# A decoder layer on one core: the first attention scores computed in 32x32 blocks instead of 32x128 strips

## The chip, the cores and the metric

The kernel runs on one core of one Trainium2 chip. Its time is the device time of one execution in microseconds (us); the figure for a version is the median over its runs. A core has five engines that run side by side: TensorE (PE in the profile; its weight loads are listed apart as PEld), VectorE (DVE), ScalarE (ACT), GpSimd (POOL) and SyncE (SP, which here issues the DMAs). A score is a number from a product of queries and keys; PSUM is the memory that TensorE writes to, SBUF the one that it reads from.

## The reference

One decoder layer over 128 sequences of 128 positions and width 256: self-attention, cross-attention over a context, and a feed-forward part with ternary weights, each behind a layer norm and added to x.

```python
x = x + attn(layernorm(x), Wq, bq, Wk, bk, Wv, bv, Wo, bo)             # 16 heads of 16
x = x + xattn(layernorm(x), ctx, ctx, mask, wq, wk, wv, wo, biases)    # 16 heads of 16
x = x + ffn(layernorm(x), W_fc, ln_w, ln_b, W_proj)                    # 256 -> 1024 -> 256

# both attentions, for one sequence and head
scores = Q @ K.T / sqrt(16)
scores = where(mask == 0, 1e-09, scores)      # cross-attention only; one mask for all sequences
out = softmax(scores) @ V
```

All inputs and the output are float32.

## The kernel before

The sequences are worked in 32 groups of 4. Each sequence passes through self-attention and through cross-attention; the kernel calls one sequence in one of them a row, so there are 256 rows, 128 self and 128 cross, four of each in turn.

Scores are computed twice in a row. The first scores have the queries on the partitions; only the largest of each query and head is taken from them, so that the exponentials can be shifted. The second scores have the keys on the partitions; they are exponentiated and multiplied with the values. The change touches the first scores.

The steps of a row, in the order in which `attention` (L680) issues them:

- `maxima` (L542): the first scores of the following row, and their maxima. 16 heads lie as 4 strips of 32 partitions (r), 2 chunks (o) and 2 heads in each strip (e). `qt` holds the queries as columns, 128 partitions x 2 chunks x 512 tokens; `kt` holds the keys of the two heads of a strip in two copies, each with the other head's rows set to zero, so one product of 32 rows gives 2 heads x 128 keys. For each o and r, L562 multiplies 32 rows x 128 queries (`qt[strip, o, tok]`, the weights that are loaded) with 32 rows x 256 columns of keys: 8 products, into a score tile of 128 queries, in two PSUM tiles of two banks each, `s[0]` for strips 0 and 1 and `s[1]` for 2 and 3. In a cross row, L551 first writes -1e30 where a key is masked: sixteen bf16 products of 32 rows and 32 columns (an identity) with 512 columns of `never`, one for each strip r and block of 32 queries c; L562 then adds onto them. DVE takes the maxima of the two tiles (L573) and lays them out as `negm` (L579, L584).
- `outputs` (L656): the exponentials of the row before, times the values: 16 products of 128 rows and 32 columns (L665), copied out by ACT (L668).
- `transposed_scores` (L611): the second scores, 16 products of 32 rows and 128 columns (L620), in the same two PSUM tiles as the first scores (pool `ps_s`, two buffers).
- `transposed_maxima` (L587): the maxima of the following row, transposed (L589) and laid out for the second scores (L594, or L604 and L606).
- `weights` (L637): in a cross row the maxima are added by 16 more products (L644); ACT takes the exponentials (L653).

Between these steps stand the steps of other groups: projections of queries, keys and values (L266, L278), output projections (`po`, L278), transposes (L246, L414), the feed-forward products (L385, L437). A string of letters, `ORDER` (L50), fixes how they alternate: "A" is one piece of `attention`, and "n", "k", "c", "f" are pieces of the preparation of self-attention, of the cross keys, of cross-attention and of the feed-forward part. The program issues its instructions in that order, and each engine takes its own in order, so TensorE's sequence is fixed by hand.

The score tiles pass from step to step: first scores (PE), maxima (DVE), second scores (PE), exponentials (ACT), first scores of the next row. Each product that is first in a PSUM tile waits until the reader before has finished: the first product of strip 0 for `s[0]`, the first of strip 2 for `s[1]`.

A float32 product is one call in the program and two instruction pairs (a weight load and a matmul) on the chip; a bf16 or fp32r product is one pair. The instruction stream has the two pairs of a product one behind the other.

## Time and profile before

| | before |
|---|---|
| median of 3 runs | 2844.08 us (2841.91 to 2845.41) |
| the profiled execution | 2845.54 us |
| its span, first to last instruction | 2843.5 us |
| mean granted TensorE clock | 0.98 |
| matmuls and weight loads | 32797 each |
| first scores (L562): matmuls, union of their time | 4096, 301.2 us |
| the mask's products (L551): matmuls, union of their time | 2048, 64.8 us |
| first scores' maxima (L573, DVE): instructions, mean | 512, 1215 ns |
| exponentials (L653, ACT): instructions, mean | 512, 1023 ns |
| instruction fetches (queue q8) | 259 pieces, 4.24 MB |

How to read a group line: the source line, engine and operation, then the tile written and the tiles read, for a matmul its rows*columns in the array, the partitions x elements that stream, and the count; behind the first bar the busy time (us) and the mean duration of one (ns); behind the second the engine's idle time just before these instructions, and what ended it. A matmul's duration overlaps with its neighbours', because matmuls are pipelined; what a group costs is read from the start of its first matmul to the start of the next group's. A line of the chain that ended last gives a start (us), a length (us) and the work. A timeline line gives the start and the length of a merged group, and how many instructions of it had begun in the stretch asked for.

### The profile page before, as it was taken

The numbers are of one execution on the slowest core, as the hardware profiler recorded it, in microseconds if no ns is written. First come the engines' busy times: TensorE is split into PE (matmuls) and PEld (weight loads), VectorE is DVE, ScalarE is ACT, GpSimd is POOL, SyncE is SP. The second block draws the span as 40 slices with busy tenths as digits, with TensorE's granted clock in tenths as the row PEclk, the third lists the DMA queues.
The fourth block names the chain that finished last, engine by engine and source line by source line (L and its number), as shares of the span: only waits on it lengthen the run. The fifth ranks groups of instructions, "written<-read, shape, count | busy, mean of one in ns | idle before, by whom it ended". The sixth has DMA issues, their size and how long they took to land.

```text
span 2843.5 us, 76860 instructions
## 1 busy us (share of the span) xinstructions
PE 2723.7 (96%) x32797; PEld 1965.4 (69%) x32797; DVE 2045.6 (72%) x3788; ACT 1546.9 (54%) x2369; POOL 1371.8 (48%) x1425
## 2 busy tenths in 40 slices
PE   4789999999999999999999999999999999999985
PEld 2456777777777777777777777777777777777664
DVE  4457777787777778777777877777777777787663
ACT  0245555655655565555556556555655655566443
POOL 1225455554545555454545545454544545455343
PEclk8799999999999999999999999999999999999988
DMA  2112211211221121122112112211211221121111
GB/s 82 31 32 48 55 37 43 56 44 44 56 55 33 47 55 40 47 55 55 33 47 55 40 47 55 56 32 49 55 40 47 55 54 32 49 52 33 43 24 31
DMA packets 110948, 131.38 MB, mean 46 GB/s; under 512 B 32657, under 2 KB 69393, under 8 KB 110609
## 3 DMA queue, kind: packets, MB, share of 16 engines
q1 hardware_dynamic: 110608, 126.48, 18.2%
q8 instruction: 259, 4.24, 0.6%
q14 instruction: 81, 0.66, 0.1%
HBM read 71.91 MB, written 18.87 MB: 32 GB/s over the span
## 4 chain that ended last, share of the span: by engine, by line
PE 93%; DVE 3%; DMA 1%; POOL 1%; issue 1%; ACT 1%; SPq 0%; POOLq 0%; ACTq 0%; DVEq 0%
PE st L620 10%; PE s L562 10%; PE av L665 9%; PE py L437 9%; PE po L278 9%; PE ph L385 8%; PE pv L278 8%; PE pq L266 8%; PE pk L266 8%; PE pg L414 4%; PE pt L246 3%; PE st L644 3%; PE s L551 2%; PE pn L589 1%; DVE mx L573 1%
## 5 line engine op out<-in xcount | busy, mean ns | idle before, releaser
L573 DVE TENSOR_REDUCE mx<-s 128x8 f32<-128x1024 f32 x512 | 600.7, 1215 | 73.7 <-PE s L562 71.5
L653 ACT ACTIVATE w_t<-st 128x1024 f32<-128x1024 f32 x512 | 496.6, 1023 | 223.5 <-PE st L620 195.6
L223 POOL TENSOR_SCALAR rstd<-agg 128x4 f32<-128x4 f32 (+1 forms) x160 | 38.1, 238 | 1172.2 <-DVE agg L218 1170.3
L228 POOL TENSOR_SCALAR xn<-x,agg,rstd 128x256 f32<-128x256 f32 x384 | 464.2, 1221 | 10.0
L630 DVE COPY_PREDICATED_SCALAR st<-masked_t,masked_score 128x1024 f32 x256 | 315.7, 1279 | 64.5 <-PE st L620 61.0
L422 ACT ACTIVATE g<-pg,ln_w 128x256 fp32r<-128x256 f32 x512 | 211.4, 477 | 214.4 <-PE pg L414 211.0
L668 ACT COPY raw<-av 128x512 f32<-128x512 f32 x256 | 150.0, 586 | 302.9 <-PE av L665 302.6
L562 PE MATMUL s<-kt,qt 32*128 32x256 f32 x4096 | 301.2, 406 | 1.7 <-ACT w_t L653 1.7
L356 POOL TENSOR_TENSOR o_raw<-o_raw,factors 128x256 f32<-128x256 f32 x256 | 178.8, 726 | 252.5 <-DMA factors<-by_head 196.6
L665 PEld LDWEIGHTS av<-w_t,v 128*32 128x32 f32 x8192 | 211.6, 110 | 118.0 <-issue 26.0
L665 PE MATMUL av<-w_t,v 128*32 128x128 f32 x8192 | 281.2, 278 | 7.2 <-DVE negm_t L606 1.5
L228 POOL TENSOR_SCALAR g<-g,agg,rstd 128x1024 f32<-128x1024 f32 x64 | 276.8, 4324 | 6.7
L385 PE MATMUL ph<-w_fc,xn 128*128 128x512 f32 x1024 | 275.1, 411 | 1.2 <-ACT g L392 1.2
L437 PE MATMUL py<-w_proj,g 128*128 128x256 f32 x2048 | 272.2, 289 | 0.3 <-DVE g L424 0.2
L437 PEld LDWEIGHTS py<-w_proj,g 128*128 128x128 f32 x2048 | 254.9, 194 | 14.7 <-issue 9.6
L562 PEld LDWEIGHTS s<-kt,qt 32*128 32x128 f32 x4096 | 189.1, 187 | 108.1 <-issue 58.3
L424 DVE SCALAR_TENSOR_TENSOR g<-pg,ln_w,g 128x256 fp32r<-128x256 f32 x512 | 216.8, 476 | 32.0 <-ACT g L422 30.0
L385 PEld LDWEIGHTS ph<-w_fc,xn 128*128 128x128 f32 x1024 | 188.6, 192 | 55.2 <-DVE g L228 9.6
L314 DVE COPY v<-pv 128x512 f32<-128x512 f32 x128 | 86.3, 674 | 149.5 <-PE pv L278 149.5
L594 DVE SCALAR_TENSOR_TENSOR q_max<-pn,max_rows,qt 128x256 f32<-128x256 f32 x256 | 110.6, 474 | 111.8 <-PE pn L589 111.8
L392 ACT ACTIVATE g<-ph 128x512 f32<-128x512 f32 x256 | 146.2, 597 | 65.0 <-PE ph L385 64.2
L360 DVE TENSOR_TENSOR x<-x,po 128x512 f32<-128x512 f32 x128 | 87.5, 684 | 120.2 <-PE po L278 120.2
(113 smaller groups left out, 4748.6 us busy)
## 6 DMA issues: line engine op xcount, KB each, us to landing
o_raw<-raw SPq DMA_DIRECT2D x512, 64.0 KB
factors<-by_head SPq DMA_DIRECT2D x128, 256.0 KB
x<-in_x_dram SPq DMA_DIRECT2D x32, 512.0 KB
ctx_t<-in_ctx_t_dram SPq DMA_DIRECT2D x32, 512.0 KB
out_dram<-x SPq DMA_DIRECT2D x32, 512.0 KB
sums<-raw SPq DMA_DIRECT2D x128, 16.0 KB
by_head<-r SPq DMA_DIRECT2D x64, 32.0 KB
raw<-in_w_fc_t_dram SPq DMA_DIRECT2D x1, 1024.0 KB
```

What stands on the lines that cost most here:

```text
L228: engine.tensor_scalar(dst[:, j], src[:, j], agg[:, j, 0:1], rstd[:, j : j + 1], ALU.subtract, ALU.mult)
L266: nc.tensor.matmul(out, w[:, c, o * P : (o + 1) * P], src_t[:, c], start=(c == 0), stop=(c == CC - 1))
L278: nc.tensor.matmul(rows[:, j], src_t[:, c, (j0 + j) * P : (j0 + j + 1) * P], w[:, c], start=(c == 0), stop=(c == CC - 1),)
L385: nc.tensor.matmul(ph, xn_parts[i][:, c, (j0 + j) * P : (j0 + j + 1) * P], w_fc[:, c, n * 512 : (n + 1) * 512], start=((i, c) == terms[0]) ...
L424: nc.vector.scalar_tensor_tensor(parts[1][:, f0 + f], pieces[:, f], scales[f], parts[0][:, f0 + f].bitcast(F32), ALU.mult, ALU.subtract,)
L437: nc.tensor.matmul(rows[:, j], parts[i][:, f, j * P : (j + 1) * P], w_proj[:, f], start=((i, f) == terms[0]), stop=((i, f) == terms[-1]),)
L562: nc.tensor.matmul(s[r // 2][:, r % 2, 2 * o : 2 * o + 2], qt[strip, o, tok], kt[strip, o, :, tok], start=(stage == "self"), stop=True, sk ...
L573: nc.vector.tensor_reduce(mx[:, 2 * half : 2 * half + 2], s[half], AX.X, ALU.max, negate=True)
L620: nc.tensor.matmul(s[r // 2][:, r % 2, n], kt[strip, n // 2, n % 2, tok], added[strip, n // 2, n % 2] if stage == "self" else qt[strip, n ...
L630: nc.vector.copy_predicated(s[half].rearrange("p r n q -> p (r n) q"), masked_t[:, None, :].to_broadcast([P, 8, P]), masked_score[:, :, No ...
L653: nc.scalar.activation(w_t[:, 2 * half : 2 * half + 2], s[half], AF.Exp)
L665: nc.tensor.matmul(av[32 * r : 32 * r + 32, n], v[:, j, head : head + 32], w_t[:, r, n], start=True, stop=True)
```

## The change

The 8 products of 32 rows and 128 queries become 32 products of 32 rows and 32 queries: a loop over c, the block of 32 queries, is added around the loop over r, as L551's products already have it, and both now take their slices from one list, `BLOCKS`. Each product loads 32 columns of `qt` as weights and streams the same 256 columns of keys, into 32 partitions of the score tile. The order is: for each o, for each c, for each r. L551's products keep their operands and order. Everything else stays.

```diff
+BLOCKS = [
+    (r, slice(r * 32, (r + 1) * 32), c, slice(c * 32, (c + 1) * 32)) for c in range(S4) for r in range(S4)
+]
...
         if stage == "cross":
-            for c in range(S4):
-                for r in range(S4):
-                    strip = slice(r * 32, (r + 1) * 32)
-                    nc.tensor.matmul(
-                        s[r // 2][c * 32 : (c + 1) * 32, r % 2],
-                        ident_b[strip],
-                        never[strip, c, None, :].to_broadcast([32, 4, P]),
...
+            for r, strip, c, block in BLOCKS:
+                nc.tensor.matmul(
+                    s[r // 2][block, r % 2],
+                    ident_b[strip],
+                    never[strip, c, None, :].to_broadcast([32, 4, P]),
...
         for o in range(CC):
-            for r in range(S4):
-                strip = slice(r * 32, (r + 1) * 32)
+            for r, strip, c, block in BLOCKS:
+                queries = slice(j * P + block.start, j * P + block.stop)
                 nc.tensor.matmul(
-                    s[r // 2][:, r % 2, 2 * o : 2 * o + 2],
-                    qt[strip, o, tok],
+                    s[r // 2][block, r % 2, 2 * o : 2 * o + 2],
+                    qt[strip, o, queries],
                     kt[strip, o, :, tok],
                     start=(stage == "self"),
                     stop=True,
```

More of the change, by code (lines that the diff above doesn't have):

```diff
@@ L547, in maxima @@
         if stage == "cross":
-            for c in range(S4):
-                for r in range(S4):
-                    strip = slice(r * 32, (r + 1) * 32)
-                    nc.tensor.matmul(
-                        s[r // 2][c * 32 : (c + 1) * 32, r % 2],
-                        ident_b[strip],
-                        never[strip, c, None, :].to_broadcast([32, 4, P]),
-                        start=True,
-                        stop=False,
-                        skip_group_check=True,
-                    )
+            for r, strip, c, block in BLOCKS:
[3 more added lines that the diff above has]
+                    never[strip, c, None, :].to_broadcast([32, 4, P]),
+                    start=True,
+                    stop=False,
+                    skip_group_check=True,
+                )
         for o in range(CC):
-            for r in range(S4):
-                strip = slice(r * 32, (r + 1) * 32)
+            for r, strip, c, block in BLOCKS:
+                queries = slice(j * P + block.start, j * P + block.stop)
                 nc.tensor.matmul(
-                    s[r // 2][:, r % 2, 2 * o : 2 * o + 2],
-                    qt[strip, o, tok],
+                    s[r // 2][block, r % 2, 2 * o : 2 * o + 2],
+                    qt[strip, o, queries],
                     kt[strip, o, :, tok],
```

## The prediction

> **What bounds the kernel now.** I read the page's busy row and slices first, then the busy time by stretches, the chain that ended last, and the timeline around one row of scores.

> ```profile
> PE 2723.7 (96%) x32797; PEld 1965.4 (69%) x32797; DVE 2045.6 (72%) x3788; ACT 1546.9 (54%) x2369; POOL 1371.8 (48%) x1425
> ...
> PE   4789999999999999999999999999999999999985
> ...
> PEclk8799999999999999999999999999999999999988
> ...
> PE 93%; DVE 3%; DMA 1%; POOL 1%; issue 1%; ACT 1%; SPq 0%; POOLq 0%; ACTq 0%; DVEq 0%
> ```
> ```profile
> 110.00:2600.00 2490.00, 2465.65 (x30340) 1779.76 (x30342) 1856.69 (x3408) 1419.33 (x2166) 1254.79 (x1298) 1.00 0.19 47
> ```
> TensorE is the bound: in the stretch of 2490 us (columns: length, then PE, PEld, DVE, ACT and POOL busy) it is busy 2465.65 us, 99%, at granted clock 1.00. What the change does to TensorE's own time is what it does to the kernel; DVE, next, has a quarter of that stretch free. So the question is how long a row of first scores holds TensorE. The chain gives it piece by piece (start, us, what), and the trace's groups give the kinds of product:

> ```profile
> 1490.06 0.11 PE pn L589
> 1490.17 0.36 PE s L551 x16
> 1490.53 1.08 PE s L562 x16
> 1491.61 1.91 PE pq L266 x4
> 1493.52 1.01 PE av L665 x32
> ```
> ```profile
> L562 PE MATMUL s<-kt,qt 32*128 32x256 f32 x4096 | 301.2, 406 | 1.7 <-ACT w_t L653 1.7
> ...
> L665 PEld LDWEIGHTS av<-w_t,v 128*32 128x32 f32 x8192 | 211.6, 110 | 118.0 <-issue 26.0
> ...
> L562 PEld LDWEIGHTS s<-kt,qt 32*128 32x128 f32 x4096 | 189.1, 187 | 108.1 <-issue 58.3
> ```
> A row's 8 products are 16 matmuls: each float32 product runs as two parts, A and B, each with its own weight load (4096 = 256 rows x 16). The 0.36 us ahead of them is L551's sixteen bf16 products, in the 128 cross rows only. In the timeline the row starts like this, four at once, one for each strip:

> ```profile
> 1490.10 0.43 PE L551 MATMUL s<-never,ident_b 32*32 32x512 bf16 x16
> 1490.46 0.50 PE L562 MATMUL s<-kt,qt 32*128 32x256 f32 x4
> ```
> By the trace's single starts (medians over the rows), the four waves begin at 0, 320, 536 and 752 ns, the next group's first matmul at 1076. A wave is 216 ns of streaming; the first is 104 longer, the load of 128 weight columns that nothing covers; the end holds 216 and some 108 before a matmul of another tile shape starts. That last is a price of the shape: after L266's 512 columns the next starts at 429 ns if it is 128x128 as well (L589) and at 522 if it is 32x128 (L562), 93 more.

> **The change, part by part.** It removes 8 products a row and puts 32 in their place: 12288 more matmuls and as many weight loads (4096 become 16384 of each), on TensorE alone; no instruction of another engine and no DMA is added or moved, and the waits still sit on the row's first and third product (on L551's in cross rows).

> *Streaming: 0.* Each 32x32 block gets four parts of 216 ns (two o, A and B). If all sixteen blocks run side by side, that is the four waves of now. What speaks for it: L551 starts its sixteen within 50 ns (3.35 apart) and is done at 365, so four column blocks on one strip overlap; L665 streams float32 on four column blocks at once, its waves 109 ns apart for 128 columns, the same rate per column as now. And a waiting B does not hold back the next block's A: strips r0 to r3 start 7 ns apart (two parts of 3.35), though r0's B stands between r0's A and r1's A in the program.

> *Weight loads: -79 ns a row.* L665 loads 32 columns (110 ns mean against 187); its first wave is 25 ns longer than the later ones (134 against 109), where the s row's is 104. 104 - 25 = 79.

> *Spreading of the starts: +80 ns a row.* The last block has 15 products of two parts ahead of it, 15 x 6.7 = 100 ns where the fourth strip now starts after 20. Self rows: 1076 - 79 + 80 = 1077, nothing. Bounds: -79 if the late start costs nothing; above, the sequencer's own pace bounds it: it passes the 65 instructions between two of its recorded waits (L665, L278) in 344 ns, 5.3 each, so 21.2 a product, 318 ns for the last block, +298 for +80, or +218 a row. I take +80, as the first 32 parts fit what the queue holds: the wait behind L620's 32 parts is passed 29 ns after the first of them starts.

> *The shape switch between L551 and L562: the gain.* Both are now 32x32. A block's first s product can follow its L551 product, with its weights loaded underneath. From L551's start: 50 (spread) + 25 (load) + 216 (its 512 bf16 columns) + 4 x 216 + 88 (304 from the last start to the next group, less 216) = 1243, where it was 365 + 1076 = 1441. Gain 198 ns x 128 cross rows = 25.3 us. A change of type alone costs no drain where the trace shows one: L385 (fp32r, 512 columns) to L278 (float32), both 128x128, starts after 228. Bf16 to float32 at one shape does not occur; the ends are 0 and 198, I take 198.

> *Code: 0.* 4.24 MB came in 259 pieces; 24576 instructions of 64 B are 96 more. A piece takes 1.07 us (median), one comes each 10.4 us and would each 8; the shortest gap now is 6.2. [...]

> *A late second half.* When r2's wait on ACT (L653) holds, fewer products now stand ahead of it (2 of 32 for 2 of 8). Only some 4 of 256 rows show strips r0 and r1 starting alone in L562: under 1 us.

> *What the rest gives back.* TensorE's order is fixed; a wait that has under 0.2 us to spare and spans a cross row eats part. An example: at 1505.767 L620 starts 0.08 us after DVE's second maximum (1505.69), so 0.12 of the 0.2 us would be lost there, once in each of 32 groups: 3.8 us. Of 25.3 I keep 22 (bounds 12 and 25).

> Sum: the profiled execution took 2845.54 us (span 2843.5, 2.0 around it); -22 makes 2823.5. The median of the runs, 2844.08, is 1.5 below it: **2822**. The case's own range is 2810 (both best ends, 25.3 + 79 ns x 128 self rows = 10.1) to 2835.

> [...]

> **Rivals.** *1, slower: sixteen at once is not what happens.* The place is the queue in front of the array. Now, r3's A overtakes a load 11 instructions older (r0's B); afterwards, the last block's A (the 61st) must overtake c0 r0's waiting B (the 4th), a reach of 58, and no row of the trace shows more than 11. If the reach is about 32, two column blocks start at first and o=0 and o=1 together take five waves for four: 216 x 256 = 55.3 us, less the 25.3: 2874. If it is not much above 11, one column block's B runs beside the next one's A, nine waves for four: 5 x 216 x 256 = 276 - 25 = +251, 3095. It decides from 25.3 / 256 = 99 ns a row on, half a wave. For it: the trace shows four in flight and no more wherever products have two parts (L551's have one). Against: the queue takes all of L620's 64 instructions, and strips that start apart (L620 at 1494.46 and 1494.61) go on independently. The slow pace of issue (above) is the mild form: 218 ns x 128 + 79 x 128 (cross rows, whose last block would start at 370 for 291) = 38 - 25 = +13, 2857.
> *2, no change: bf16 to float32 drains like a change of shape.* Then cross rows are 365 + 1077: 2844. For it, no such pair is in the trace; against it, L385 to L278.
> *3, a third of it: waits take more.* If every cross row has a chain like the one at L620, 128 x 0.12 = 15.4 are lost and 10 stay: 2834. Against: TensorE idles only 24 us in those 2490.

> **How the numbers follow.** About 0.2% (5.7 us) is what a measurement here can tell from no change. Forecast 0.54 and rival 3 0.05: faster 0.59. Rival 2 and what falls near it: 0.09. Rival 1: 0.32, of which 0.18 for its mild and middle forms (2850 to 2890) and 0.14 for nine waves. The predicted time is the forecast's. The range runs from 2810 to 2890: below it 0.04, above it the 0.14, so it holds about 0.82.

> **What would show it.** Right: L562's matmuls 16384, sixteen starting within some 110 ns, waves 216 apart; a self row 1.08 us in the chain as now; a cross row's L551 and L562 together 1.24 for 1.44, with no gap of 100 ns between them; PE busy some 25 us down. Wrong: starts in groups of four with 216 between them (rival 1, nine waves), a fifth wave, or a start spacing above 7 ns; a gap of 75 ns or more between L551's end of streaming and L562 (rival 2); unchanged L551 and L562 gains but more idle before L620 or L644 (rival 3).

## The result, and the profile after

The changed kernel takes 2910.97 us (median of 6 runs, 2905.70 to 2912.12), the kernel before 2842.99 over its 6: the ratio is 1.024, with a 95% interval of 1.0226 to 1.0254. One of the six runs of the kernel before took 3413.41 us; the other five lie between 2838.81 and 2845.41. It is 2.4% slower, where 2822 us was forecast with a range to 2890.

The page of the changed kernel, the lines that answer to those shown of before (first scores are now L565, their mask's products L554, the outputs L668, the second scores L623):

```profile
span 2909.0 us, 101436 instructions
...
PE 2793.3 (96%) x45085; PEld 2006.6 (69%) x45085; DVE 2046.8 (70%) x3788; ACT 1547.7 (53%) x2369; POOL 1374.5 (47%) x1425
...
PE   4789999999999999999999999999999999999985
...
PEclk8899999999999999999999999999999999999988
...
PE s L565 12%; PE st L623 10%; PE av L668 9%; PE py L442 9%; PE po L283 8%; PE ph L390 8%; PE pv L283 8%; PE pk L271 8%; PE pq L271 8%; PE pg L419 4%; PE pt L251 3%; PE st L647 3%; PE s L554 2%; PE pn L592 1%; DVE mx L576 1%; DVE st L633 1%
...
L565 PE MATMUL s<-kt,qt 32*32 32x256 f32 x16384 | 402.4, 390 | 1.7 <-ACT w_t L656 1.6
...
L565 PEld LDWEIGHTS s<-kt,qt 32*32 32x32 f32 x16384 | 246.9, 104 | 117.9 <-issue 30.2
```

TensorE is still the bound (busy 96% of the span, as before) and its mean granted clock is the same, 0.98; its busy time grew by 69.6 us (2723.7 to 2793.3) and the span by 65.5. The first scores carry that: their union of time goes from 301.2 to 402.4 us (with the mask's products, which they now overlap in the cross rows, from 357.1 to 433.9), while DVE, ACT and POOL did the same work as before. Measured in the trace from a row's first matmul to the next group's, all rows together take 429.6 us for 358.4: +71.2, and the other groups give back 5.7 of it.

The chain that ended last shows a self row (1501.62) and a cross row (1518.45):

```profile
1500.75 0.87 PE pt L251 x8
1501.62 1.42 PE s L565 x60
1503.04 2.10 PE py L442 x16
...
1518.34 0.11 PE pn L592
1518.45 0.36 PE s L554 x16
1518.82 1.21 PE s L565 x48
```

A self row holds TensorE for 1.42 us where it was 1.08. That self row in three stretches of the timeline, one behind the other (a line counts the instructions of its group that ran in the stretch asked for):

```profile
1501.55 0.50 PE L565 MATMUL s<-kt,qt 32*32 32x256 f32 x16
1501.55 0.21 PEld L565 LDWEIGHTS s<-kt,qt 32*32 32x32 f32 x29 [0.17 <-issue]
```
```profile
1501.55 0.83 PE L565 MATMUL s<-kt,qt 32*32 32x256 f32 x33
1502.01 0.10 PEld L565 LDWEIGHTS s<-kt,qt 32*32 32x32 f32 x1
```
```profile
1501.82 0.82 PE L565 MATMUL s<-kt,qt 32*32 32x256 f32 x17
1502.19 0.15 PEld L565 LDWEIGHTS s<-kt,qt 32*32 32x32 f32 x6
```

The first stretch ends at 1501.66: sixteen matmuls have started. The second is 1501.90 to 1502.18: in 0.28 us a single weight load begins, though the blocks' second parts began at 1501.79, and beside the first parts' streaming the next loads had begun at once (29 of them in the first stretch, for sixteen matmuls). The third begins at 1502.19: now the loads come. In single starts from the row's first (medians over the self rows): part A of the sixteen blocks of o=0 at 0 to 102 ns, part B at 242 to 342, the first product of o=1 at 458, and then nothing more of o=1 until 647, from where one product follows another every 16.6 ns. The row ends at 1424 instead of 1076.

What starts late begins with instruction 69 of the row's 128 (32 products, two parts each, a load and a matmul for each part). In a cross row, where 32 instructions of the mask stand ahead, the late ones begin halfway through o=0, at the third column block: the matmul of its first part A is the 66th instruction, and starts at 413 ns.

### The profile page after: what moved, and what is told of

It is laid out like the page before. It is cut to its first block, busy times and chain, and to the rows that moved or that the text cites. A ratio compares the mean times of both kernels' runs of the same rounds, so it can differ in the third digit from the quotient of the medians.

```text
span 2909.0 us, 101436 instructions
## 1 busy us (share of the span) xinstructions
PE 2793.3 (96%) x45085; PEld 2006.6 (69%) x45085; DVE 2046.8 (70%) x3788; ACT 1547.7 (53%) x2369; POOL 1374.5 (47%) x1425
## 2 busy tenths in 40 slices
PE   4789999999999999999999999999999999999985
## 4 chain that ended last, share of the span: by engine, by line
PE 93%; DVE 3%; DMA 1%; POOL 1%; SPq 1%; ACT 1%; issue 1%; ACTq 0%; DVEq 0%; POOLq 0%
PE s L565 12%; PE st L623 10%; PE av L668 9%; PE py L442 9%; PE po L283 8%; PE ph L390 8%; PE pv L283 8%; PE pk L271 8%; PE pq L271 8%; PE pg L419 4%; PE pt L251 3%; PE st L647 3%; PE s L554 2%; PE pn L592 1%; DVE mx L576 1%; DVE st L633 1%
## 5 line engine op out<-in xcount | busy, mean ns | idle before, releaser
L565 PE MATMUL s<-kt,qt 32*32 32x256 f32 x16384 | 402.4, 390 | 1.7 <-ACT w_t L656 1.6
L671 ACT COPY raw<-av 128x512 f32<-128x512 f32 x256 | 150.2, 587 | 343.8 <-PE av L668 343.5
L565 PEld LDWEIGHTS s<-kt,qt 32*32 32x32 f32 x16384 | 246.9, 104 | 117.9 <-issue 30.2
L668 PEld LDWEIGHTS av<-w_t,v 128*32 128x32 f32 x8192 | 209.7, 110 | 123.0 <-issue 66.0
L668 PE MATMUL av<-w_t,v 128*32 128x128 f32 x8192 | 279.2, 277 | 3.5 <-DVE negm_t L609 1.2
```

Source lines behind the costliest of these rows:

```text
L565: nc.tensor.matmul(s[r // 2][block, r % 2, 2 * o : 2 * o + 2], qt[strip, o, queries], kt[strip, o, :, tok], start=(stage == "self"), stop= ...
L668: nc.tensor.matmul(av[32 * r : 32 * r + 32, n], v[:, j, head : head + 32], w_t[:, r, n], start=True, stop=True)
```

## The experiments

The theory that these numbers suggested, called "queue" below, is the author's picture of the start times: the runs show when an instruction starts, not what holds it. In the picture TensorE's queue holds 64 instructions, a place comes free in program order, and what takes it starts some 0.41 us later (in the self row 647 - 242 ns). Rivals: every extra instruction costs the same wherever it stands ("pace"), or the narrow shapes themselves make a second product wait or stream slower ("blocks"). Times are medians in us, ratios against the kernel before in the same runs.

| kernel | time | ratio, 95% interval | self row, ns | cross row, ns |
|---|---|---|---|---|
| before | 2842.99 | 1 | 1076 | 1441 |
| the change | 2910.97 | 1.024, 1.0226 to 1.0254 | 1424 | 1701 |
| e1, eight blocks of 64 | 2839.66 | 0.9989, 0.998 to 0.9998 | 1049 | 1414 |
| e2, column block by column block | 3086.13 | 1.0858, 1.0838 to 1.0879 | 2155 | 2357 |
| e3, change in self rows only | 2888.88 | 1.0164, 1.0145 to 1.0183 | 1425 | 1440 |
| e4, change in cross rows only | 2868.58 | 1.0091, 1.0077 to 1.0104 | 1076 | 1702 |
| e5, sixteen blocks, 64 instructions, self rows | 2845.56 | 1.0011, 1.0002 to 1.0021 | 1071 | |
| e6, the same in all rows | 2847.01 | 1.0015, 1.0007 to 1.0024 | 1071 | 1496 |
| e7, eight blocks of 64, 128 instructions | 2852.28 | 1.0028, 1.0011 to 1.0044 | 1136 | 1500 |
| e8, sixteen blocks, 256 instructions | 3058.83 | 1.0772, 1.0741 to 1.0803 | 1832 | 2108 |

A row's length runs from its first matmul (the mask's in a cross row) to the next group's first: the median for self rows, for cross rows that of rows undisturbed by a wait for ACT (the shortest tenth of them; in the middle one, a cross row of before takes 1619). It is left blank for e5's cross rows, which are unchanged.

### e1: eight blocks of 64 queries

```diff
-            for r, strip, c, block in BLOCKS:
-                queries = slice(j * P + block.start, j * P + block.stop)
+            for c in range(2):
+                block = slice(c * 64, (c + 1) * 64)
+                queries = slice(j * P + block.start, j * P + block.stop)
+                for r in range(S4):
```

> Eight blocks of 64 queries at once in place of sixteen of 32: 16 products, 32 parts, 64 instructions a row, just what stands in TensorE's queue. Theory (queue: a row's 65th and later instructions come some 0.41 us after the queue's head moves on, so only rows of more than 64 instructions stall): no stall, four waves of 216 follow each other at once; self row 1076 - 104 + 52 (load of 64 columns) + 27 (spread of eight starts) = 1051, cross row 365 + 1051; 25 ns x 256 = 6 us less than before, about 2837. Rival (pace: each extra matmul and weight load costs the same 67 us / 12288 = 5.5 ns, wherever it stands): 4096 extra, +22 us, 2865. Rival (blocks: a block's second product waits for something in the narrow shapes themselves): waves 3 and 4 late by 190 ns as in the changed kernel, +40 us, 2885.

Measured 2839.66 us, ratio 0.9989 (0.998 to 0.9998), and this is the chain around one of its self rows:

```profile
1521.85 0.86 PE pk L271 x2
1522.71 1.05 PE s L568 x32
1523.76 1.01 PE av L671 x32
```

1.05 us, as worked out; the four waves follow each other at once (starts at 0, 267, 482 and 698 ns). Both rivals, at +22 and +40 us, fall. 4096 extra matmuls cost nothing, and half the exposed weight load is gained (the second wave starts at 267 ns for 320): the self row is 27 ns shorter than before. In time that is 0.11% under the kernel before, no more than the difference that e5 below shows without a cause in its rows.

### e2: both o of a column block before the next

```diff
-        for o in range(CC):
-            for r, strip, c, block in BLOCKS:
+        for c in range(S4):
+            block = slice(c * 32, (c + 1) * 32)
...
+            for o in range(CC):
+                for r in range(S4):
```

> The same 32 products a row in another order: both o of a column block before the next column block. Theory (queue, freed in program order): the first 64 instructions are two column blocks, whose last parts start at about 700 ns; the third block's o=0 comes at 650, its o=1 and the fourth block only from about 1100; a self row of about 2.1 us where the changed kernel has 1.42, cross rows a little less; +0.6 to +0.7 us x 256, about 3060 to 3090. Rivals (pace, or blocks): the same number of instructions and the same shapes, about 2911.

Measured 3086.13 us; the chain of its trace:

```profile
1512.99 0.11 PE pn L595
1513.10 2.15 PE s L568 x60
1515.25 1.02 PE pt L251 x8
```

A self row takes 2.15 us with the same 128 instructions of the same shapes that took 1.42. Only their order differs: the first 64 now belong to 8 blocks, and the other 8, by the theory, have to wait for places. Pace and blocks both asked for no change and are out.

### e3 and e4: the change in one kind of row

```diff
+        if stage == "self":        # e4: "cross"
+            blocks = BLOCKS
+        else:
+            blocks = [(r, slice(r * 32, (r + 1) * 32), 0, slice(0, P)) for r in range(S4)]
         for o in range(CC):
-            for r, strip, c, block in BLOCKS:
+            for r, strip, c, block in blocks:
```

> The sixteen blocks in self rows alone; cross rows as before. Theory (queue): a self row takes 1424 ns for 1076, 348 x 128 = 44.5 us more, about 2887. Rival (pace): half the extra instructions, half of the 67 us, 2876.

> The sixteen blocks in cross rows alone; self rows as before. Theory (queue): the mask's products and the scores follow without the drain (227 ns to the first score for 365), then the stall; 1701 ns for 1441 of an undisturbed row of before, but rows of before that wait for ACT give up to 178 back: +11 to +33 us, 2854 to 2876, by the means of the two traces (1847 for 1635) +27, 2870. Rival (pace): 2876 less 17 for the drain that is saved, 2859.

Measured 2888.88 and 2868.58 us: +47 and +27 over the 2841.53 of before in these runs. Pace's 2876 and 2859 lie outside the intervals (lower ends 2841.53 x 1.0145 = 2883 and x 1.0077 = 2863). Together the two parts make +74, the whole change +68: they add up within what the intervals leave. The self rows, which have nothing to gain, carry most of the loss; in the cross rows the drain that is saved (in the trace of the change the first score starts at 227 ns, before at 365) pays for part of the stall, and the mean row, which in the kernel before holds waits for ACT, grows by 212 ns (1635 to 1847 in the traces of the kernel before and the changed one) where the undisturbed one grows by 260.

### e5 and e6: sixteen blocks at once with 64 instructions

Both kernels leave out the second chunk's scores, e5 in the self rows, e6 in all rows; each product streams the first chunk's keys twice.

```diff
+            for r, strip, c, block in BLOCKS:
+                queries = slice(j * P + block.start, j * P + block.stop)
+                nc.tensor.matmul(
+                    s[r // 2][block, r % 2].rearrange("p (o e) k -> p o e k", o=CC),
+                    qt[strip, 0, queries],
+                    kt[strip, 0, None, :, tok].to_broadcast([32, CC, 2, P]),
```

> Left out: the second chunk's scores in self rows; each product streams the first chunk's 256 key columns twice, 512 in all. So a self row has the same sixteen blocks at once, the same float32 streaming on each (864 ns), but 16 products, 64 instructions. Theory (queue): nothing comes late; 100 (spread) + 25 (load) + 864 + 88 = 1077 ns a self row, as before; time as before, within 0.2%. Rival (pace: 5.5 ns for each extra matmul): 2048 extra, +11 us. Rival (sixteen blocks of float32 stream slower than four strips): the two waves take longer than 432 each, and up to the 348 ns that the changed kernel's self row lost, +44 us.

> The same in all rows (second chunk's scores left out everywhere). Cross rows: the mask's 16 products are 32 instructions, so the scores' last 32 of 64 stand behind the queue's end. Theory (queue): the first score starts 227 ns after the mask's first, as in the changed kernel, the 66th instruction comes at some 413 ns and the last block's product at 546; 546 + 25 + 864 + 88 = 1523 ns a cross row against 1441 undisturbed before, 1701 in the changed kernel; as rows of before wait up to 178 ns for ACT, the time moves between -10 and +10 us. Without a limit of the queue it would be 1243, -25 us or, with the waits, -48.

Measured 2845.56 and 2847.01 us. A self row is 1071 ns in both; one of e5 in the chain, and behind it a cross row of e6:

```profile
1523.61 0.86 PE pk L271 x2
1524.47 1.07 PE s L565 x32
1525.54 1.03 PE av L680 x32
```

```profile
1515.38 1.84 PE ph L390 x8
1517.22 0.37 PE s L554 x16
1517.59 1.13 PE s L565 x32
1518.72 2.04 PE ph L390 x8
```

Sixteen float32 blocks stream as fast side by side as four strips do: with 64 instructions a self row takes 1071 ns for 1076. The change's own idea works on the array; it is the number of instructions that it takes that does not (128 of them, 1424 ns). The cross row, 96 instructions with the mask's, is late again, which the theory puts down to what stands behind the first 64 (0.37 + 1.13 = 1.50 here, 1243 without a limit). e5 is 0.11% over before where its rows are 5 ns shorter; that difference has no cause in the rows and is left open.

### e7: the theory's first form fails

```diff
+        for n in range(4):
+            for c in range(2):
+                block = slice(c * 64, (c + 1) * 64)
...
-                    s[r // 2][block, r % 2, 2 * o : 2 * o + 2],
+                    s[r // 2][block, r % 2, n],
...
-                    kt[strip, o, :, tok],
+                    kt[strip, n // 2, n % 2, tok],
```

> Eight blocks of 64 queries, and each product streams 128 key columns in place of 256: the same streaming on each block (8 waves of 109 ns), but 32 products, 128 instructions a row, in blocks that did not stall with 64. Theory (queue of 65, freed in program order, refilled 406 ns later at 16.6 ns a product): the third quarter of the products comes from 566 ns on instead of 488, the last from 785; a row takes about 1243 ns against 1049 with 64 instructions and 1076 before; 167 x 256 = 43 us over before, about 2886. Rival (pace, 5.5 ns for each extra matmul): as many instructions as the changed kernel, 2910. Rival (only blocks of 32 columns stall): the row is about 1050, 2840.

Measured 2852.28 us; a self row in the chain:

```profile
1478.63 0.11 PE pn L595
1478.74 1.14 PE s L568 x63
1479.88 1.02 PE pt L251 x8
```

There is a stall, in blocks of 64 columns, so "only blocks of 32 columns stall" is out; but a row takes 1136 ns, not 1243. The single starts say why: instruction 69 comes at 460 ns, right behind the 68th, which in the theory takes the place of the 4th, the matmul of the first block's part B. That one started at 162, so 298 ns pass and not 406. The difference of 108 is that of the streaming, 216 against 109. Counted from the end of that matmul's streaming the delay is the same in both: 647 - (242 + 216) = 189 and 460 - (162 + 109) = 189. So the theory is mended: a place is free when its matmul has finished, not when it starts.

### e8: a fresh test of the mended form

The edit is shown against e7:

```diff
-            for c in range(2):
-                block = slice(c * 64, (c + 1) * 64)
+            for c in range(S4):
+                block = slice(c * 32, (c + 1) * 32)
```

> Sixteen blocks of 32 queries, and each product streams 128 key columns: 64 products, 256 instructions a row, the same streaming on each block (8 waves of 109). Theory as mended after the row of 1136 ns (a place in the queue of 64 comes free, in program order, when its matmul has streamed to its end, and the instruction 64 further on can start 187 ns later, at 16.6 ns a product): worked through instruction by instruction, a self row of 1833 ns and a cross row of 2111; with 120 to 146 ns of waits and start-up in the mean cross row, as the other narrow kernels had, (1833 - 1076) x 128 + (2111 + 133 - 1635) x 128 = 175 us, about 3018. Theory as it was (free when the matmul starts, 406 ns later): a self row of 2150, 3090 or more.

Measured: self row 1832 ns, cross row 2108, the mended form's 1833 and 2111; the first form's 2150 falls. The chain shows a self row:

```profile
1497.99 0.11 PE pn L595
1498.10 1.83 PE s L568 x101
1499.93 1.02 PE pt L251 x8
```

Worked back, the mended form gives 1426 and 1704 for the changed kernel's rows (1424 and 1701), 2157 and 2360 for e2 (2155 and 2357), 1051 for e1 (1049), 1077 and 1504 for e6 (1071 and 1496) and 1137 for e7 (1136). The single starts also settle the theory's count of 64. The first matmul of the 17th product is instruction 66. Its block is free at 242 ns, but it starts at 318, which is 185 after instruction 2, the first part A, has streamed (133); in a theory with 65 places it would have taken that of the first load and been in time.

The kernel's time, 3058.83, is 41 us over the forecast 3018, and the trace shows where that lies. Between 240 and 2600 us, 14 cross rows pause for 0.5 to 1.75 us, 15 us together, which lifts the mean cross row to 2367 ns from the 2244 forecast. Another 20 pauses, 23 us together, stand in other groups, 18 of them behind an output product (L671). All 34 end 1.2 to 1.6 us after an instruction fetch has landed; 483 pieces came, for 259 in the kernel before. Neither that kernel nor the changed one has such a pause in this stretch. That the fetches cause them is likely, but was not tested.

## Why the prediction was wrong

The direction was wrong. Point by point, by its own steps:

- *Streaming, 0:* right. e5's row has the same streaming on sixteen blocks and takes 1071 ns.
- *Weight loads, -79 ns:* right in size. The changed kernel's second parts begin 242 ns after its first, 216 of them streaming, so some 25 of load are left of 104.
- *Spreading of the starts, +80 ns:* this is the step that failed. Its own numbers hold for the first 32 parts, which start 6.7 ns apart and reach 102 ns for the last block. But it took "the first 32 parts fit what the queue holds" as enough, and bounded the rest by the sequencer's pace of 5.3 ns an instruction. The parts of o=1 start late: the first at 458, when the first part B has streamed, the next only 189 ns later, and from there one product comes every 16.6 ns. The self row ends at 1424 for the 1077 forecast, so the term was +427 and not +80; its upper bound, +298, did not reach that, because it had a pace and no delay.
- *The shape switch, -198 ns a cross row:* right, and nearly in size: the first score starts 227 ns after the mask's first product, as the trace of the changed kernel has it, for 365 before and 241 forecast; no drain shows between bf16 and float32 at this one shape, and rival 2 is out. The gain is there and is then spent: the same row ends at 1701 for the 1243 forecast, 458 later, by the same late starts (the 66th instruction at 413).
- *Code, 0:* right. 355 pieces of 16384 B came, 96 more, which is 64 B for each of the 24576 instructions, and no row of the changed kernel pauses at one. What would hide a fetch no run shows; at e8's 483 pieces pauses do follow fetches.
- *What the rest gives back:* small, and of the other sign, as the rows became longer: the other groups took 5.7 us less. Which of their waits shrank was not traced.
- *Rival 1* had the slower side right, at 0.32, and by the theory the place (the queue ahead of the array). Its mechanism was another: a reach within the queue. The reach is long enough, since the last block's part A started at 102 ns past 15 waiting parts; late is what stands behind the first 64 instructions, which the theory puts down to the queue's capacity and to places that come free only from the front (the same 128 instructions in e2's order take 2155 ns for 1424). Its prices, 2857, 2874 and 3095, belong to mechanisms that the runs did not show.

The trace of before could hardly show it: but for two places, its runs of narrow products of one shape are at most 64 instructions (L665, L620), and these stream for some 870 ns (8 waves of 109), so a delay of 189 would be covered. The prediction's own reading for the first half of the row, that the wait behind L620's 64 instructions is passed 29 ns after the first of them starts, is not in the trace: in the 247 rows where such a wait is recorded, none passes it less than 346 ns after. The first 64 instructions fit all the same, as e1 and e5 show. The prediction counted the 64 instructions of L620 as taken by the queue (rival 1); what a row of 128 does behind them it did not ask.

## What to carry to other kernels

When a change splits products into smaller ones that run side by side, count the instructions that TensorE gets between two changes of tile shape (a float32 product is four here, two loads and two matmuls: 16384 of each for the change's 8192 products). In these runs a split up to 64 was free (e1 and e5, ratios 0.9989 and 1.0011) and could gain part of the exposed weight load (e1's self row, 27 ns); beyond that, the late instructions started only some 0.19 us after a matmul 64 or 65 instructions ahead had finished streaming, so what stands behind the first 64 has to be covered by longer streams in fewer products (e5 for the change, a self row of 1071 ns for 1424), wider blocks (e7 for e8: 1136 for 1832), or an order that lets the front finish early (the change for e2: 1424 for 2155). Where four strips stream as fast as sixteen blocks, as here (1076 and 1071 ns), a finer split has only the load and the drain to win (104 ns exposed in the first wave, 365 - 227 before the first score).
